# High scheduling priority for six DVE and ACT passes in a one-core, four-layer graph-network kernel

## The chip, the core and the metric

The kernel runs on one core of a Trainium2 chip. The metric is device time in microseconds (us) from launch to end; the median of three runs of the kernel before is 2236.18 us (2234.99 to 2238.05). The engines are TensorE (PE in the profile, with its weight loads shown as PEld), VectorE (DVE), ScalarE (ACT), GpSimd (POOL) and SyncE (SP). PE writes its products to PSUM, and DVE and ACT read them from there; POOL works in SBUF alone.

## The reference

128 graphs of 64 nodes with 256 features each go through four layers. Every layer ends in a residual and a LayerNorm.

```python
x = layernorm(x + L0(x, adj))   # five node groups (25, 9, 7, 6, 6 nodes): GCN 256->512->256, weighted sum
x = layernorm(x + L1(x, adj))   # D^-1/2 (adj + I) D^-1/2  x W + b
x = layernorm(x + L2(x, adj))   # sum_k conv_w[k] * An^k (x W^T) + conv_b, leaky ReLU; An = adj / row sum
x = layernorm(x + L3(x, adj))   # five rounds: m = h W_l; agg = A01^T m; h = GRU(agg, h)
```

Layer 2 is a polynomial in the normalised adjacency `An`. Layer 3 runs a gated recurrent cell five times: gates r and z are sigmoids, n is a tanh, and the new state is `(1 - z) n + z h`.

## The kernel before

**Tiling.** Layer 0 goes by 16 units of up to four tiles of graphs (`prep`, `aggregate`, `hidden`, `support`, `add`, `finish`). From layer 1 on the work goes by 16 chunks of eight graphs, held as four pairs of 128 nodes (`NP = 4`), so most tiles are 128 x 512 values of float32.

**Layers 1 and 2** of a chunk are the generator `mid(c)`. It builds `Ab` (two adjacencies as one block-diagonal 128 x 128), `An` and `dg` on DVE. Then it makes the layer-2 polynomial by Horner's rule: a transpose of `Ab` on PE (L255) and a DVE pass into `poly3` (L257); a product `An x poly` on PE into `pp` (L265) and a DVE pass that reads `pp` and writes `poly1` (L267); a second product on PE, with `poly1` as its operand (L272), and a DVE pass into `poly0` (L274). Between the two products stands `gather(xt, AT1)`: 16 matmuls into `pa` (L209) in two halves, each copied to SBUF by ACT (L212), and after it the DVE pass L269 on `xt`. A `yield` in `mid` marks where the caller may go on with something else.

**Layer 3** is the main loop over 80 steps (16 chunks of five rounds, two chunks in turn). A step `s` does the gates of one chunk (`x.rz`, `x.n`) while the other (`w`) finishes its round: `w.n(4)` and `w.n(3)` end in `update`, whose DVE passes L803 to L805 write the new state `hn`; `w.turn` transposes it on PE (L745) and `w.close` calls `messages`, which is `gather` into `agg` (L209, L212) and `sums` on POOL (`Ta`, L684 to L686; `Th` from `hn` in the same way). Each gate product is Strassen-like: seven products (numbers 1 to 7), whose partial sums in a PSUM bank are copied by ACT (L721) and added by DVE (L723, L727, L733). ACT then applies the sigmoids (L771, L773, L775) and the tanh (L802, in `update`). DVE's `reset` (L797, L798) stands in front of the tanh.

**What sets the order.** PE's order is written out by hand (`manual_schedule` for PE, L325): PE runs its instructions as the program text lists them. The order on DVE, ACT and POOL is chosen by a scheduler when the kernel is built: roughly, among the instructions that it takes as ready it issues the one that comes first in the program text, except that those traced under `tc.high_priority()` go first. Two passes have that priority already: the copies of partial sums (L721) and of the transposed state (L819). In layer 3 `next(filler)` runs one stage of `mid` of a later chunk in two places of each step, in PE's order after `x.rz(6)` and after `x.n(5)`. So the Horner stage (L265, gather, L272) falls between `x.rz(6)` and `x.rz(5)`, while DVE still works on `w.n(4)` and `w.n(3)`.

**PSUM.** Two pools: `pg` with five banks (gates) and `pt` with three (everything that `psum` allocates: `pT`, `pp`, `pa`, `pd`). The scheduler also decides which freed `pt` bank a new tile gets.

Of the kernel before, what the change touches and what calls it, by code (L numbers as in the profile page):

```python
# [11 lines left out]
ALU = mybir.AluOpType  # L12
# [55 lines left out]
def gnn_stack(  # L68
# [26 lines left out]
    nc = tc.nc  # L95
# [13 lines left out]
    def spread(src, n, name, pool=wp, eng=None):  # L109

        return const(bass.AP(tensor=src.tensor, offset=src.offset, ap=[[0, 128], [1, n]]), [128, n], name, eng, pool)

    powers, evictions = [], []

    def inv_sqrt(v, n, p, name):

        z = small.tile([p, n], F32, name=name + "z")
        nc.vector.tensor_scalar(z, v, 0.0, None, op0=ALU.is_equal)
        s = small.tile([p, n], F32, name=name + "s")
        nc.vector.tensor_add(s, v, z)  # L120
        r = small.tile([p, n], F32, name=name + "r")
        powers.append(nc.gpsimd.tensor_tensor(r, s, mhalf[:p, :n], ALU.pow))
        o = small.tile([p, n], F32, name=name + "o")
        nc.vector.scalar_tensor_tensor(o, v, 0.0, r, op0=ALU.not_equal, op1=ALU.mult)
        return o
# [51 lines left out]
    def psum(name):  # L177
        return pt.tile([128, 512], F32, tag="pt", name=name)

    def psum0(name):  # L180

        taken[0] += 1
        if taken[0] % 8 < 5:
            return pg.tile([128, 512], F32, tag="pg", name=name)
        return psum(name)
# [17 lines left out]
    def gather(src, m, name, pool=keep, tag="ag", bufs=1):  # L203

        a = pool.tile([128, 2, NP * 128], F32, tag=tag, name=name, bufs=bufs)
        for k in range(2):
            p = psum("pa")
            for q in range(NP):
                nc.tensor.matmul(  # L209
                    p[:, q * 128 : (q + 1) * 128], src[:, q, k * 128 : (k + 1) * 128], m[:, q, :], start=True, stop=True  # L210
                )
            nc.scalar.copy(a[:, k, :], p)  # L212
        return a

    adjs, xts = {}, {}
# [2 lines left out]
    def mid(c):  # L218
# [22 lines left out]
        dg = keep.tile([128, NP, 128], F32, name="dg", bufs=1)  # L241
# [3 lines left out]
        poly = keep.tile([128, NP, 128], F32, tag="poly", name="poly3", bufs=2)  # L245
# [7 lines left out]
        p = psum("pT1").rearrange("p (q n) -> p q n", q=NP)  # L253
        for q in range(NP):
            nc.tensor.transpose(p[:, q, :], Ab[:, q, :], ident)  # L255

        nc.vector.scalar_tensor_tensor(poly, p, cw[:, 3:4], poly, op0=ALU.mult, op1=ALU.add)  # L257

        nc.vector.tensor_add(AT1, p, ident[:, None, :].to_broadcast([128, NP, 128]))
        nc.vector.tensor_mul(AT1, AT1, dinv1[:, :, None].to_broadcast([128, NP, 128]))  # L260
# [2 lines left out]
        p = psum("pp").rearrange("p (q n) -> p q n", q=NP)  # L263
        for q in range(NP):
            nc.tensor.matmul(p[:, q, :], An[:, q, :], poly[:, q, :], start=True, stop=True)  # L265
        poly = keep.tile([128, NP, 128], F32, tag="poly", name="poly1", bufs=2)
        nc.vector.scalar_tensor_tensor(poly, dg, cw[:, 1:2], p, op0=ALU.mult, op1=ALU.add)  # L267
        ag = gather(xt, AT1, "ag1")
        nc.vector.tensor_add(xt, xt, l1bs[:, None, :].to_broadcast([128, NP, D]))  # L269
        p = psum("pp").rearrange("p (q n) -> p q n", q=NP)  # L270
        for q in range(NP):
            nc.tensor.matmul(p[:, q, :], An[:, q, :], poly[:, q, :], start=True, stop=True)  # L272
        poly = keep.tile([128, NP, 128], F32, tag="poly", name="poly0", bufs=2)
        nc.vector.scalar_tensor_tensor(poly, dg, cw[:, 0:1], p, op0=ALU.mult, op1=ALU.add)  # L274
        yield
        for u in range(NP // 2):
            p = psum("pd").rearrange("p (q d) -> p q d", q=2)
# [15 lines left out]


        ag = gather(xt, poly, "ag2")
        yield
        for u in range(NP // 2):
            p = psum("pd").rearrange("p (q d) -> p q d", q=2)
# [6 lines left out]
            v = keep.tile([128, 2, D], F32, name="v", bufs=1)  # L305
# [22 lines left out]
    with ExitStack() as c0:  # L328
# [29 lines left out]
        def prep(i):  # L358

            u = UNITS[i]  # L360
            a, xg = loads.pop(i)
            ae = work.tile([TR, 4, NJ], F32, name="ae", bufs=2)
            A0 = work.tile([TR, 4, TR], F32, name="A0", bufs=1)
            AT = work.tile([TR, 4, TR], F32, name="AT", bufs=4)
            p = psum0("pT").rearrange("p (t n) -> p t n", t=4)
            scale = []
            for ts, nb, r, k in u.same:
                w, c = ts.stop - ts.start, 0
                for f, m in [(0, u.n)] if u.g < 2 else RUNS[u.g]:
                    nc.vector.tensor_add(  # L370
                        ae[:r, ts, c : c + m], a[:r, ts, f : f + m], eye0[:r, k, None, c : c + m].to_broadcast([r, w, m])
                    )
                    c += m
                av = ae[:r, ts, : u.n]
                deg = small.tile([TR, w], F32, name="deg")
                nc.vector.tensor_reduce(deg[:r], av, AX.X, ALU.add)
                dinv = inv_sqrt(deg[:r], w, r, "d0")
                nc.vector.tensor_mul(av, av, dinv[:, :, None].to_broadcast([r, w, u.n]))
                o, c = 0, 0
                for _, m in RUNS[u.g]:  # L380
                    nc.vector.tensor_mul(
                        A0[:r, ts, o : o + nb * m].rearrange("p t (b n) -> p t b n", n=m),
                        ae[:r, ts, None, c : c + m].to_broadcast([r, w, nb, m]),
                        block0[:r, None, k, o : o + nb * m].rearrange("p t (b n) -> p t b n", n=m)
                        .to_broadcast([r, w, nb, m]),
                    )
                    o, c = o + nb * m, c + m
                for t in range(ts.start, ts.stop):
                    nc.tensor.transpose(p[:r, t, :r], A0[:r, t, :r], ident[:r, :r])
                scale.append((AT[:r, ts, :r], p[:r, ts, :r], dinv[:, :, None].to_broadcast([r, w, r])))  # L390
            for v in scale:
                evictions.append(nc.vector.tensor_mul(*v))
            A[i] = AT, xg

        def aggregate(i):
            u = UNITS[i]
            AT, xg = A[i]
            ag0 = work.tile([128, 2, 512], F32, name="ag0", bufs=2)
            for k in range(2):
                p = psum0("pa0")  # L400
                for t, r in enumerate(u.rows):
                    nc.tensor.matmul(  # L402
                        p[:, u.off[t] : u.off[t] + r], xg[:r, t, k * 128 : (k + 1) * 128], AT[:r, t, :r],
                        start=True, stop=True,
                    )
                nc.scalar.copy(ag0[:, k, : u.cols], p[:, : u.cols])
            AG[i] = ag0

        def hidden(i):
# [125 lines left out]
        def products(l, q):  # L535
# [7 lines left out]
            return p  # L543

        early = both(mid(0), mid(1))

        places = [(1, 1), (1, 2), (2, 1), (2, 2), (2, 2), (3, 1), (3, 2), (3, 2)]
# [11 lines left out]
        for i in range(-2, NU + 1):  # L559
# [3 lines left out]
            if i:  # L563
                stage(aggregate, i + 1)
            early_stage(i, 0)
            stage(support, i)
            if not i:
                aggregate(1)
# [4 lines left out]
            if i == -1:  # L573

                hidden(0)
                with tc.issue_after(evictions[0].ins):
                    prep(1)
            else:
                stage(prep, i + 2)
                stage(hidden, i + 1)  # L580
# [33 lines left out]
            elif i == 1:  # L614
                with tc.issue_after(powers[-1].ins):
                    pair = const_later(c_pair, [128, 2, N], "pair")
                    cw = spread(conv_w, 4, "cw", eng=nc.gpsimd)
# [117 lines left out]
    class Chunk:  # L735
# [20 lines left out]
        def messages(self, h=None):  # L756
            self.agg = gather(self.xt if h is None else h, self.A01, "agg", work, "agg", 2)
            self.ta = sums(self.agg, "a")
# [95 lines left out]
    for s in range(NCH * L):  # L854
        u, t = s // (2 * L) * 2, s % (2 * L)
        if t == 0:
            for _ in filler:
                pass
            if u + 2 < NCH:
                for c in (u + 2, u + 3):  # L860
                    load_adj(c)
                    load_x(c)
                filler = both(mid(u + 2), mid(u + 3))
# [104 lines left out]
```

## Time and profile before

| engine | busy us | share of the span |
|---|---|---|
| PE | 2184.9 | 98% |
| PEld | 1912.4 | 86% |
| DVE | 1402.4 | 63% |
| ACT | 1003.4 | 45% |
| POOL | 596.4 | 27% |

The profiled execution spans 2234.4 us and its mean granted PE clock is 0.995. PE is busy without a break over almost all of it, so the useful numbers are those of its idle time: 49.5 us in all (2234.4 less 2184.9). In time the kernel has a start-up of some 20 us, layer 0 until about 345 us, the main loop from there, in which `mid` runs beside layer 3 until about 1960 us, and a tail after PE's last long stretch at about 2200 us.

How to read the profile's lines. A row of the waits gives the engine and line that waited, whom it waited for, the total us, how many times, and the longest. A row of the timeline gives the start, the duration, the engine, the line of the kernel, the operation with output and inputs, how many instructions are merged, and in brackets how long the engine had been idle before it and what ended that. Instructions of DVE that follow each other overlap a little in such rows: one shown with 0.68 us is followed by the next 0.60 us after its start.

### The profile page before, as it was taken

The numbers are of one execution on the slowest core, as the hardware profiler recorded it, in microseconds if no ns is written. First come the engines' busy times: TensorE is split into PE (matmuls) and PEld (weight loads), VectorE is DVE, ScalarE is ACT, GpSimd is POOL, SyncE is SP. The second block draws the span as 40 slices with busy tenths as digits, with TensorE's granted clock in tenths as the row PEclk, the third lists the DMA queues.
The fourth block names the chain that finished last, engine by engine and source line by source line (L and its number), as shares of the span: only waits on it lengthen the run. The fifth ranks groups of instructions, "written<-read, shape, count | busy, mean of one in ns | idle before, by whom it ended". The sixth has DMA issues, their size and how long they took to land.

```text
span 2234.4 us, 30150 instructions
## 1 busy us (share of the span) xinstructions
PE 2184.9 (98%) x11526; PEld 1912.4 (86%) x11526; DVE 1402.4 (63%) x3068; ACT 1003.4 (45%) x1850; POOL 596.4 (27%) x639
## 2 busy tenths in 40 slices
PE   7999999999999999999999999999999999999997
PEld 5677788888888888888888888888888888888886
DVE  4443666675766666666756676757666666566546
ACT  2333334445545444445444454455454544455443
POOL 3210123222223223223222232222222232232222
PEclk9999999999999999999999999999999999999998
DMA  6531110000100000000100010001000000000000
GB/s 188 170 124 31 48 46 4 1 3 1 41 1 3 1 20 22 3 1 11 31 1 3 1 41 1 4 1 41 1 1 1 20 10 1 1 10 10 1 1 20
DMA packets 54172, 51.12 MB, mean 23 GB/s; under 512 B 20878, under 2 KB 49036, under 8 KB 54028
## 3 DMA queue, kind: packets, MB, share of 16 engines
q1 hardware_dynamic: 49524, 43.90, 6.4%
q0 software_dynamic: 1936, 4.83, 0.7%
q8 instruction: 91, 1.49, 0.3%
q10 hardware_dynamic: 2568, 0.47, 0.1%
q14 instruction: 53, 0.43, 0.1%
HBM read 32.40 MB, written 16.78 MB: 22 GB/s over the span
## 4 chain that ended last, share of the span: by engine, by line
PE 86%; DVE 7%; DMA 2%; issue 2%; POOL 1%; SPq 1%; ACT 0%; ACTq 0%; POOLq 0%; DVEq 0%
PE parz L704 23%; PE pdrz L704 12%; PE pan L704 12%; PE pa L209 8%; PE pdn L704 6%; PE pbrz L704 6%; PE pT L745 4%; PE pbn L704 3%; PE ph L416 3%; PE ps L430 3%; PE pd L281 2%; PE pd L302 2%; DMA xo<-in_x_dram 1%; PE pp L272 1%; PE pa L402 1%
## 5 line engine op out<-in xcount | busy, mean ns | idle before, releaser
L704 PE MATMUL parz<-Th,WHH 128*128 128x256 f32 x960 | 285.8, 379 | 0.0
L704 PE MATMUL parz<-Ta,V 128*128 128x256 f32 x960 | 285.5, 379 | 0.0
L684 POOL TENSOR_TENSOR Th<-hn 128x512 f32<-128x512 f32 x64 | 85.8, 1340 | 722.3 <-DVE hn L805 657.5
L721 ACT COPY c<-parz 128x512 f32<-128x512 f32 x240 | 140.8, 586 | 305.9 <-PE parz L704 305.1
L802 ACT ACTIVATE NI<-NI,bih 128x512 f32<-128x512 f32 x160 | 115.3, 721 | 224.3 <-DVE NI L798 224.3
L721 ACT COPY c<-pan 128x512 f32<-128x512 f32 x240 | 141.1, 588 | 150.7 <-PE pan L704 150.7
L704 PEld LDWEIGHTS parz<-Ta,V 128*128 128x128 f32 x960 | 182.4, 190 | 24.8
L684 POOL TENSOR_TENSOR Ta<-agg 128x512 f32<-128x512 f32 x80 | 104.6, 1307 | 345.4 <-ACT agg L212 345.4
L704 PEld LDWEIGHTS parz<-Th,WHH 128*128 128x128 f32 x960 | 176.2, 190 | 20.9 <-ACT c L721 0.2
L775 ACT ACTIVATE RZ<-RZ,brz 128x512 f32<-128x512 f32 x160 | 106.7, 714 | 138.3 <-DVE RZ L733 138.3
L733 DVE TENSOR_TENSOR RZ<-pdrz,c 128x512 f32<-128x512 f32 x80 | 55.0, 688 | 176.2 <-PE pdrz L704 176.2
L704 PE MATMUL pan<-Ta,V 128*128 128x256 f32 x480 | 143.1, 380 | 0.9 <-ACT c L721 0.9
L704 PE MATMUL pan<-Th,WHH 128*128 128x256 f32 x480 | 142.8, 379 | 0.0
L727 DVE TENSOR_TENSOR NI<-pbn,c 128x512 f32<-128x512 f32 x80 | 55.3, 692 | 127.7 <-PE pbn L704 125.3
L138 POOL TENSOR_TENSOR rs<-ve,mhalf 128x4 f32<-128x4 f32 (+2 forms) x66 | 68.1, 1032 | 242.9 <-DVE ve L136 235.6
L723 DVE TENSOR_TENSOR NI<-pdn,c 128x512 f32<-128x512 f32 x80 | 55.2, 689 | 115.3 <-ACT c L721 115.3
L209 PEld LDWEIGHTS pa<-A,h 128*128 128x128 f32 x1024 | 124.4, 192 | 3.3
L209 PE MATMUL pa<-A,h 128*128 128x128 f32 x1024 | 124.6, 275 | 0.0
L803 DVE TENSOR_TENSOR RZ<-hn,NI 128x512 f32<-128x512 f32 x128 | 87.9, 687 | 48.5 <-ACT NI L802 48.4
L805 DVE TENSOR_TENSOR hn<-RZ,NI 128x512 f32<-128x512 f32 x160 | 109.7, 686 | 1.8
L804 DVE TENSOR_TENSOR RZ<-RZ 128x512 f32<-128x512 f32 x160 | 109.5, 685 | 1.8
L797 DVE SCALAR_TENSOR_TENSOR NI<-NI,bhh,RZ 128x256 f32<-128x256 f32 (+1 forms) x160 | 105.1, 657 | 2.0
(199 smaller groups left out, 5107.6 us busy)
## 6 DMA issues: line engine op xcount, KB each, us to landing
out_dram<-xt SPq DMA_DIRECT2D x32, 256.0 KB
W<-in_w_dram SPq DMA_DIRECT2D x10, 512.0 KB
xt<-xb SPq DMA_DIRECT2D x32, 156.0 KB
xo<-in_x_dram SPq DMA_DIRECT2D x9, 512.0 KB
xb<-xo SPq DMA_DIRECT2D x9, 512.0 KB
xt<-xa SPq DMA_DIRECT2D x32, 100.0 KB
xg<-in_x_dram SPq DMA_DIRECT2D x25, 125.0 KB
xa<-xg SPq DMA_DIRECT2D x25, 125.0 KB
```

Source lines behind the costliest of these rows:

```text
L138: nc.gpsimd.tensor_tensor(rs[:r, :n], ve[:r, :n], mhalf[:r, :n], ALU.pow)
L209: nc.tensor.matmul(p[:, q * 128 : (q + 1) * 128], src[:, q, k * 128 : (k + 1) * 128], m[:, q, :], start=True, stop=True)
L684: nc.gpsimd.tensor_sub(t[:, 0:2, :], a[:, :, H:], a[:, 0, :].rearrange("p (s n) -> p s n", s=2))
L704: nc.tensor.matmul(bank[:, g, :], w[:, q, i - 1, :], rhs, start=i in (1, 2, 5) and g == 0 and m == 0, stop=m == len(side) - 1, skip_group_ ...
L721: nc.scalar.copy(c, self.a)
L745: nc.tensor.transpose(p[:, q * 128 : (q + 1) * 128], src(q, k), ident)
L775: nc.scalar.activation(RZ[:, q, 0, :], RZ[:, q, 0, :], AF.Sigmoid, bias=b[0])
L797: nc.vector.scalar_tensor_tensor(n[:, j, f], h, bhh[:, 4 + j : 5 + j], r[:, j, f], op0=ALU.add, op1=ALU.mult)
L802: nc.scalar.activation(n, n, AF.Tanh, bias=bih[:, 4 + j : 5 + j])
L803: nc.vector.tensor_sub(d, self.hT[:, j, :], n)
L804: nc.vector.tensor_mul(d, d, z)
L805: nc.vector.tensor_add(self.hn[:, j, :], d, n)
```

## The change

Six passes are put under `tc.high_priority()`: the ACT copies of `gather` (L212) and layer 0's `aggregate` (L406), the three polynomial passes on DVE that read PSUM (L257, L267, L274), and the scaled transposes of layer 0 (L392). The result of each is an operand of a later PE instruction. Nothing is computed differently, no instruction is added or removed, and no buffer is resized. PE's order is the same in both kernels; only the places of instructions on DVE, ACT and POOL, and with them which of the three `pt` banks a tile gets, can differ.

```diff
@@ gather
-            nc.scalar.copy(a[:, k, :], p)
+            with tc.high_priority():
+                nc.scalar.copy(a[:, k, :], p)
@@ mid
-        nc.vector.scalar_tensor_tensor(poly, p, cw[:, 3:4], poly, op0=ALU.mult, op1=ALU.add)
+        with tc.high_priority():
+            nc.vector.scalar_tensor_tensor(poly, p, cw[:, 3:4], poly, op0=ALU.mult, op1=ALU.add)
...
-        nc.vector.scalar_tensor_tensor(poly, dg, cw[:, 1:2], p, op0=ALU.mult, op1=ALU.add)
+        with tc.high_priority():
+            nc.vector.scalar_tensor_tensor(poly, dg, cw[:, 1:2], p, op0=ALU.mult, op1=ALU.add)
...
-        nc.vector.scalar_tensor_tensor(poly, dg, cw[:, 0:1], p, op0=ALU.mult, op1=ALU.add)
+        with tc.high_priority():
+            nc.vector.scalar_tensor_tensor(poly, dg, cw[:, 0:1], p, op0=ALU.mult, op1=ALU.add)
@@ prep
             for v in scale:
-                evictions.append(nc.vector.tensor_mul(*v))
+                with tc.high_priority():
+                    evictions.append(nc.vector.tensor_mul(*v))
@@ aggregate
-                nc.scalar.copy(ag0[:, k, : u.cols], p[:, : u.cols])
+                with tc.high_priority():
+                    nc.scalar.copy(ag0[:, k, : u.cols], p[:, : u.cols])
```

## The prediction

> **What bounds the kernel now.** I read the busy table first: PE 98%, everything else at 63% or less. So the end is set by PE's work plus PE's idle time, and a change of order can only act on the idle time. The second view is the busy time by stage, in whose rows the columns are the stretch, its length, and then PE, PEld, DVE, ACT and POOL.
>
> ```profile
> 0.00:20.00 20.00, 8.45 (x25) 5.81 (x26) 8.32 (x30) 2.53 (x4) 9.60 (x18) 1.00 0.83 225
> 20.00:200.00 180.00, 171.71 (x818) 127.43 (x817) 76.30 (x326) 62.78 (x107) 38.00 (x44) 0.98 0.40 125
> 200.00:360.00 160.00, 155.75 (x830) 129.22 (x829) 98.95 (x286) 57.34 (x125) 37.44 (x50) 0.99 0.15 44
> 360.00:1921.00 1561.00, 1550.84 (x8314) 1385.94 (x8313) 1033.63 (x2071) 735.16 (x1349) 428.50 (x440) 1.00 0.03 10
> 1921.00:2180.00 259.00, 259.00 (x1355) 230.51 (x1354) 149.42 (x276) 126.50 (x231) 69.80 (x76) 1.00 0.02 5
> 2180.00:2234.40 54.40, 39.14 (x194) 33.49 (x192) 35.79 (x82) 19.06 (x34) 13.05 (x12) 0.88 0.06 20
> ```
>
> Length less PE gives PE's idle time: 11.6 at the start, 8.3 and 4.2 in layer 0 and the passage to layer 3, 10.2 in the main loop while `mid` runs, 0.0 in the loop without it, 15.3 in the tail: 49.5 us. The third view says whom PE waits for.
>
> ```profile
> PE pp L272 <- DVE rinv L236: 8.5, 10, 1.5
> PE pa L402 <- DVE AT L392: 7.4, 4, 2.9
> PE pp L272 <- DVE mv L134: 1.7, 2, 1.2
> PE pp L272 <- ACT NI L802: 1.4, 1, 1.4
> PE ph L416 <- ACT ag L406: 1.3, 1, 1.3
> PE pp L272 <- DVE poly L267: 0.2, 1, 0.2
> ```
>
> The second Horner product (L272) has 8.5 + 1.4 + 0.2 = 10.1 us of it, which is all of the main loop's 10.2, and 1.7 in layer 0. The releaser named, `rinv` or `NI`, is not its input: L272 needs `poly1` of L267, and the instruction named merely ended last. The timeline of one such place shows it.
>
> ```profile
> 612.55 1.95 PE L209 MATMUL pa<-AT,xt 128*128 128x128 f32 x16
> 613.88 0.67 DVE L805 TENSOR_TENSOR hn<-RZ,NI 128x512 f32<-128x512 f32 x1
> 614.48 0.68 DVE L798 TENSOR_TENSOR NI<-NI 128x512 f32<-128x512 f32 x1
> 615.09 0.73 DVE L267 SCALAR_TENSOR_TENSOR poly<-dg,cw,pp 128x512 f32<-128x512 f32 x1
> 615.19 0.72 ACT L802 ACTIVATE NI<-NI,bih 128x512 f32<-128x512 f32 x1 [0.97 <-DVE NI L798]
> 615.96 1.13 PE L272 MATMUL pp<-poly,An 128*128 128x128 f32 x8 [1.47 <-DVE rinv L236]
> ```
>
> L267 ends at 615.82 and PE starts 0.14 later. Its input `pp` was complete by 612.7 (L265 starts at 611.65 and takes 1.05). So it stood more than 2 us behind DVE passes of the gates.
>
> **What the skill says.** The Trainium skill, "Perfetto Trace Analysis", section "Tensor Engine Instruction (MATMUL, LD_WEIGHTS)", has ACT, DVE and GPSIMD as strict FIFOs: a ready pass waits for whatever stands ahead. The stretch above agrees: DVE is busy without a gap and L267 starts 2.4 us after its input was there. "SBUF — State Buffer", section "SBUF: two separate sides", says that DVE and GpSimd share a pair of ports under an exclusive lock, so that one blocks the other for a whole instruction. The trace agrees: L118, a pass over 128x4 that takes 0.17 us elsewhere, took 1.14 at 620.78, while POOL's `Th` (L684, 1.59 us from 620.31) ran. I use this below for what the later `hn` does to POOL.
>
> **The change part by part.** I compared the built order of both kernels. PE's and SP's are identical.
>
> *L267 in the main loop (14 chunks).* It moves ahead of one pass, L798, and so starts 0.60 us earlier (614.48 in place of 615.09). The waits at L272 alternate in the two chunks of a pair: 1.47 (at 616) and 0.24 (at 712). Over seven pairs they are none and 0.24, five times 1.47 and 0.24, then 1.42 and none: 10.2 us. A wait of 0.24 goes entirely, one of 1.47 becomes 0.87, since L797 and L805 still stand ahead. Gain: 6 x 0.60 + 6 x 0.24 = 5.0 us.
>
> *L267 in layer 0 (two chunks).* It moves from behind four and three LayerNorm statistics to behind the first; at 278 that is from 277.76 to about 276.6, so it ends about 277.3, when PE is through with `pa` (278.62 less the 1.23 of its wait). Both waits, 0.51 and 1.23, go: 1.7 us. Its neighbours L153 and the stores of `xg` come about 1.5 us later there. DVE then waits 4.6 us for PE before L286 at 288.44, which hides this.
>
> *L274* moves ahead of L803 and L804. `poly0` is read by `gather` more than 20 us later: nothing gained. What is queued behind both passes: L798, and with it the tanh L802 and the second ACT copy of `pa`, 0.6 us later, and L805 for `hn`, which also falls behind L248, 0.6 us later. Readers: PE's transpose L745 of that half at 623.41, when `hn` was written by 620.2; 3.2 us of slack shrink to about 2. `pa`'s second half is read by L281 at 629.96. POOL's `Th` starts 0.6 later and in five chunks has a 1.0 us `d1r` put in between; it is needed together with `Ta`, which POOL starts only at 629.74. L723 at 621.91 can lose about 0.4 us to the port lock; its bank is written again at 624.72. Cost on PE: zero, 1 us at most per pair.
>
> *L212 for `agg` (78 moves of L775).* The order r, z, copy, copy becomes r, copy, copy, z. The copies end about 0.5 us earlier, but PE has no wait on `Ta` or `agg` in the loop, so nothing is gained. The sigmoid z (L775) is later by some 1.1 us; it is read by L804 in the next step, some 10 us on. The ACT copy behind it waits for PE anyway: 1.42 us at 2196.00 in a step without `mid`, 1.39 us at 655.29 in one with it, which is more than z's delay. In the 14 closing rounds L150 also moves behind the copies; the sum ahead of the `pan` copy stays. Cost: zero.
>
> *L406* does not move at all: the 1.3 us stay. *L392* moves in four units, all after 205 us, where PE does not wait for it; the waits of 7.4 us lie before 130 us and those passes keep their places. *L257* moves by one 0.08 us pass once. Zero each.
>
> *Banks.* L272's bank is now the one that L267 frees, where before it was one freed by an ACT copy; that copy had ended by 614.23 and did not bind. The transposes take the ACT-freed bank, 5 us later. Zero.
>
> Sum: 5.0 + 1.7 = 6.8 us; 2236.2 - 6.8 = **2229.4**.
>
> **The rivals.** (1) *Given back*: PE comes to each later place up to 0.6 us earlier while DVE, ACT and POOL have the same backlog; a wait on `hn`, on the copy of `h` (ready 1.5 us ahead of L209 at 626.44) or on a reused bank takes over. For it: DVE is gapless from 607 to 622 there. Against it: no such wait is among PE's rows, and the slacks are 1.5 us or more. If two thirds of the loop's 5.0 go, the gain is 1.7 + 1.7 = 3.4: 2232.8. (2) *All bubbles go*, because the port lock and ACT's queue resolve better as well: 10.2 + 1.7 = 11.9, so 2224.3. Against it: two long passes stay ahead of L267. (3) *Slower*: the later z or tanh makes each of the 78 reordered steps wait 0.15 us in ACT's queue at a `pan` copy, +11.7 - 6.8 = +4.9: 2241.1. For it: it would happen in every step. Against it: the 1.4 us that ACT waits for PE there, and PE's 0.0 us of idle in 259 us of loop without `mid`.
>
> **How the numbers follow.** Forecast 0.66 (2228 to 2231, with the 0.1% that the runs of before differ), rival 1 0.20, rival 2 0.06, rival 3 0.08. The range 2226 to 2235.5 takes in the forecast and rival 1 and leaves out most of the others. Over 0.2% is 4.5 us: the forecast clears it by 2.3 us, a run's spread, so I give it 0.62 of its 0.66 and some of rival 1; faster 0.73. Within 0.2%: 0.19. Slower: 0.08.
>
> **What would show it.** In the changed profile the rows of PE's waits for L272 should sum to about 5.2 us (six of 0.87) in place of 11.9, the main loop's PE idle to 5, and layer 0's two to nothing; the waits of L402 on AT stay at 7.4. L775 z stands behind the copies. A new PE row with L745, L209 or L704 waiting for DVE or ACT in the loop, in tens of times, would show rival 1 or 3.

## The result, and the profile after

The changed kernel takes 2219.03 us (median of six runs, 2217.32 to 2220.84); before, measured with it, takes 2238.31 (2234.99 to 2242.37). The ratio is 0.9914, with an interval of 0.9902 to 0.9927; a second measurement gave 2222.08 us and 0.9924 (0.9912 to 0.9937). The forecast was 2229.4 and its range ended at 2226.0: the direction was right, but the gain is 16 to 19 us where 6.8 were forecast.

**Line numbers after.** The added `with` lines shift the numbers in the profile of after. Those used below, before and after: L212 is L213, L224 is L225, L257 is L259, L260 is L262, L267 is L270, L272 is L275, L381 is L385, L389 is L393, L392 is L397, L402 is L407, L406 is L412, L416 is L422, L684 to L686 are L690 to L692, L704 is L710, L745 is L751, L775 is L781, L797 and L798 are L803 and L804, L805 is L811. L150 keeps its number. The views below show chosen rows; those between them are left out.

Busy time by stage of after (stretch, length, PE, PEld, DVE, ACT, POOL), against the rows of before with the same stretches:

```profile
200.00:360.00 160.00, 157.18 (x837) 130.62 (x836) 98.81 (x286) 57.33 (x125) 38.14 (x50) 0.99 0.15 44
360.00:1921.00 1561.00, 1561.00 (x8395) 1398.77 (x8394) 1018.58 (x2089) 743.24 (x1363) 417.81 (x443) 1.00 0.03 10
1921.00:2180.00 259.00, 259.00 (x1358) 231.09 (x1357) 146.62 (x270) 127.52 (x233) 70.64 (x77) 1.00 0.02 5
```

PE's idle time in the main loop went from 10.2 us to nothing. Look at the other columns of that row as well: DVE's busy time fell by 15 us (1033.63 to 1018.58) and POOL's by 10.7 (428.50 to 417.81), although in after slightly more of their instructions fall into this stretch (2089 for 2071, and 443 for 440). A mere change of order doesn't shorten passes; this is the first sign of what the prediction missed. PE's four largest waits of after:

```profile
PE pT L393 <- DVE A L385: 10.0, 1, 10.0
PE pa L407 <- DVE AT L397: 6.4, 4, 2.6
PE pT L751 <- DVE hn L811: 5.4, 2, 4.1
PE ph L422 <- ACT ag L412: 4.1, 1, 4.1
```

No row for the second Horner product (L275) is left, and none of the loop's gates has come in. The place that the prediction showed, in the timeline of after:

```profile
610.43 1.05 PE L267 MATMUL pp<-poly,An 128*128 128x128 f32 x8
611.22 0.68 DVE L811 TENSOR_TENSOR hn<-RZ,NI 128x512 f32<-128x512 f32 x1
611.82 0.73 DVE L270 SCALAR_TENSOR_TENSOR poly<-dg,cw,pp 128x512 f32<-128x512 f32 x1
612.48 0.68 DVE L804 TENSOR_TENSOR NI<-NI 128x512 f32<-128x512 f32 x1
613.11 0.61 PE L275 MATMUL pp<-poly,An 128*128 128x128 f32 x4
```

The order is the predicted one: `hn`, the polynomial pass, then L804. But the pass starts 1.39 us after the first product (611.82 less 610.43) where before it was 3.44 (615.09 less 611.65). One place in the order is worth 0.60 of these 2.05 us. DVE's whole backlog is shorter by about 1.4 us.

**Where the time came from.** PE runs the same 11526 matmuls in the same order in both kernels, so the distances from each matmul's start to the next can be compared one by one. In the loop (by before's times, from 345 to 2180 us) they add up to 15.4 us less:

| place in the loop | us | occurrences |
|---|---|---|
| last L209 to first L272 | 12.43 | 14 |
| first to second matmul of L272 (184 ns to 112 ns) | 1.01 | 14 |
| `parz` products on `agg` in closing rounds | 1.92 | 8, two steps each |

Layer 0's two waits at L272 add 2.0 us (1.94 to the first matmul, 0.04 inside). Other differences in layer 0 come and go between runs of the same kernel, by 2 to 3 us. The second measurement of the changed kernel has 12.43, 1.02 and 1.92 in the loop, so these terms can be relied on.

**What the prediction didn't see.** A closing round is one in which a finished chunk leaves layer 3 and a new one enters. The one ahead of the place above, first before (DVE, ACT and POOL rows of the timeline):

```profile
602.29 2.07 ACT L150 ACTIVATE xt<-xt,nb,rs 128x256 f32<-128x256 f32 x4
604.27 1.04 ACT L212 COPY agg<-pa 128x512 f32<-128x512 f32 x2
605.35 0.68 DVE L224 TENSOR_TENSOR Ab<-a,pair 128x512 f32<-128x512 f32 x1
605.39 1.77 POOL L684 TENSOR_TENSOR Ta<-agg 128x512 f32<-128x512 f32 x1 [3.33 <-ACT agg L212]
605.95 1.76 DVE L260 TENSOR_TENSOR AT<-AT,d1o 128x512 f32<-128x512 f32 x1
607.24 1.05 POOL L685 TENSOR_TENSOR Ta<-agg,Ta 128x256 f32<-128x256 f32 x1
608.37 0.86 POOL L686 TENSOR_TENSOR Ta<-agg,Ta 128x256 f32<-128x256 f32 x1
608.56 0.94 DVE L797 SCALAR_TENSOR_TENSOR NI<-NI,bhh,RZ 128x256 f32<-128x256 f32 x1
```

and then after:

```profile
600.33 1.05 ACT L213 COPY agg<-pa 128x512 f32<-128x512 f32 x2
601.46 1.29 POOL L690 TENSOR_TENSOR Ta<-agg 128x512 f32<-128x512 f32 x1 [0.64 <-ACT agg L213]
601.90 2.07 ACT L150 ACTIVATE xt<-xt,nb,rs 128x256 f32<-128x256 f32 x4
604.12 0.80 DVE L225 TENSOR_TENSOR Ab<-a,pair 128x512 f32<-128x512 f32 x1
604.84 0.68 DVE L262 TENSOR_TENSOR AT<-AT,d1o 128x512 f32<-128x512 f32 x1
606.38 0.47 DVE L803 SCALAR_TENSOR_TENSOR NI<-NI,bhh,RZ 128x256 f32<-128x256 f32 x1
```

Before, the copies of `agg` stand behind four LayerNorm passes of the finished chunk, so POOL's `Ta` begins only at 605.39, while DVE is at L224 and has L260, the second pass on `AT1`, next. `Ta`'s three passes take 1.77, 1.05 and 0.86 us in place of 1.29, 0.73 and 0.73; L260 takes 1.76 in place of 0.68, and L797, beside `Ta`'s last pass, 0.94 in place of 0.47. The ends fit a lock held for whole instructions: POOL's first pass, stretched beside L224, ends at 607.16, and DVE's 0.68 us pass, issued at 605.95, ends 0.55 later at 607.71. This is the rule of the Trainium skill ("SBUF — State Buffer", "SBUF: two separate sides") that the prediction used only for `Th`. After, the copies go first, `Ta` is through at 604.37, before L262 comes, and that pass takes 0.68 us in all 16 chunks. Before, it took 1.76 in six, 1.21 in six others, and 0.68 in the first three and the last.

In each of the six worst chunks the step from one DVE pass to the next shrinks by 1.08 us at L260 and by 0.47 at L797, and grows by 0.11 at L224, which now meets the end of `Ta`: 1.44 us together, the shorter backlog found above.

The third term was visible as well, in a view that the prediction left out. Waits of the weight-load queue (PEld) before, and one of the eight places in the timeline of before:

```profile
PEld parz L704 <- ACT agg L212: 3.0, 8, 0.4
```

```profile
582.35 1.04 ACT L212 COPY agg<-pa 128x512 f32<-128x512 f32 x2
582.40 0.59 PE L704 MATMUL parz<-hT,WHH 128*128 128x256 f32 x2
582.97 0.70 PE L704 MATMUL parz<-agg,V 128*128 128x256 f32 x2
```

The matmuls that read `agg` wait for the copy of 582.35. PE's own rows show no idle time there, because the modelled end of the product in front (582.99) lies past the start of the next.

### The profile page after: what moved, and what is told of

Read it like the earlier page. It is cut to its first block, busy times and chain, and to the rows that moved or that the text cites. A ratio compares the mean times of both kernels' runs of the same rounds, so it can differ in the third digit from the quotient of the medians.

```text
span 2218.8 us, 30141 instructions
## 1 busy us (share of the span) xinstructions
PE 2180.1 (98%) x11526; PEld 1912.2 (86%) x11526; DVE 1376.3 (62%) x3068; ACT 1004.5 (45%) x1850; POOL 582.5 (26%) x639
## 4 chain that ended last, share of the span: by engine, by line
PE 91%; DMA 3%; DVE 2%; issue 1%; SPq 1%; POOL 1%; ACT 0%; POOLq 0%; ACTq 0%; DVEq 0%
PE parz L710 25%; PE pdrz L710 12%; PE pan L710 12%; PE pa L209 9%; PE pbrz L710 6%; PE pdn L710 6%; PE pT L751 4%; PE pbn L710 3%; PE ph L422 3%; PE ps L436 3%; PE pd L285 2%; PE pd L306 2%; DMA xo<-in_x_dram 1%; PE pa L407 1%; PE po L458 1%
## 5 line engine op out<-in xcount | busy, mean ns | idle before, releaser
L710 PE MATMUL parz<-Th,WHH 128*128 128x256 f32 x960 | 285.8, 379 | 0.0
L710 PE MATMUL parz<-Ta,V 128*128 128x256 f32 x960 | 285.5, 379 | 0.0
L690 POOL TENSOR_TENSOR Th<-hn 128x512 f32<-128x512 f32 x64 | 81.6, 1274 | 774.0 <-DVE hn L811 588.5
L710 PEld LDWEIGHTS parz<-Ta,V 128*128 128x128 f32 x960 | 182.4, 190 | 24.7
L710 PEld LDWEIGHTS parz<-Th,WHH 128*128 128x128 f32 x960 | 176.2, 190 | 20.9 <-ACT c L727 0.2
L781 ACT ACTIVATE RZ<-RZ,brz 128x512 f32<-128x512 f32 x160 | 116.1, 727 | 138.6 <-DVE RZ L739 138.6
L690 POOL TENSOR_TENSOR Ta<-agg 128x512 f32<-128x512 f32 x80 | 102.2, 1277 | 260.6 <-ACT agg L213 260.6
L710 PE MATMUL pan<-Ta,V 128*128 128x256 f32 x480 | 143.2, 380 | 0.9 <-ACT c L727 0.9
L710 PE MATMUL pan<-Th,WHH 128*128 128x256 f32 x480 | 142.7, 379 | 0.0
L209 PEld LDWEIGHTS pa<-A,h 128*128 128x128 f32 x1024 | 124.4, 192 | 3.3
L209 PE MATMUL pa<-A,h 128*128 128x128 f32 x1024 | 124.6, 275 | 0.0
L811 DVE TENSOR_TENSOR hn<-RZ,NI 128x512 f32<-128x512 f32 x160 | 109.9, 687 | 1.8
L436 PE MATMUL ps<-W,hg 128*125 128x256 f32 (+5 forms) x464 | 104.2, 382 | 0.0
```

The source lines that it names most:

```text
L209: nc.tensor.matmul(p[:, q * 128 : (q + 1) * 128], src[:, q, k * 128 : (k + 1) * 128], m[:, q, :], start=True, stop=True)
L436: nc.tensor.matmul(p[: u.rows[t], t - v, :], hg[:, e, u.off[t] : u.off[t] + u.rows[t]], W2[:, u.g, e, :], start=e == 0, stop=e == 3,)
L690: nc.gpsimd.tensor_sub(t[:, 0:2, :], a[:, :, H:], a[:, 0, :].rearrange("p (s n) -> p s n", s=2))
L710: nc.tensor.matmul(bank[:, g, :], w[:, q, i - 1, :], rhs, start=i in (1, 2, 5) and g == 0 and m == 0, stop=m == len(side) - 1, skip_group_ ...
L781: nc.scalar.activation(RZ[:, q, 0, :], RZ[:, q, 0, :], AF.Sigmoid, bias=b[0])
L811: nc.vector.tensor_add(self.hn[:, j, :], d, n)
```

## The experiments

Two theories at first. A: the polynomial passes carry the whole gain, and the copies nothing, as the prediction has it. B: the copies' order sets when `Ta` runs, `Ta` slows DVE's `AT1` pass, and this delay is what keeps L267 late. Losses at L272 are from start to start, against the 0.11 us that the step takes in after.

**The polynomial passes alone** (`e1_poly`; L257, L267, L274). The edit against the whole change:

```diff
-            with tc.high_priority():
-                nc.scalar.copy(a[:, k, :], p)
+            nc.scalar.copy(a[:, k, :], p)
...
-                with tc.high_priority():
-                    evictions.append(nc.vector.tensor_mul(*v))
+                evictions.append(nc.vector.tensor_mul(*v))
...
-                with tc.high_priority():
-                    nc.scalar.copy(ag0[:, k, : u.cols], p[:, : u.cols])
+                nc.scalar.copy(ag0[:, k, : u.cols], p[:, : u.cols])
```

> Before, with the priority on the three polynomial passes alone (L257, L267, L274); ACT's order stays that of before. Theory A (the gain of the whole change comes from the place of the polynomial passes): nearly all of the 19 us, about 2220; L272 no longer waits. Theory B (half of it comes from the copies of agg, which let POOL make Ta before DVE's pass on AT1, so that the two do not block each other): AT1's pass keeps its 1.76 and 1.21 us, the long stalls at L272 shrink by 0.60 each to about 1.0 and the short ones go; 6 x 0.60 + 6 x 0.40 + some 0.9 of restarts = 6.9 us in the loop and about 1.9 in layer 0, so 8.8 less than before.

Measured: 2229.2 us (2225.57 to 2230.72), ratio 0.9955 (0.9942 to 0.9967). The row of PE's waits for the second product (L274 in this kernel):

```profile
PE pp L274 <- DVE poly L269: 4.6, 6, 0.8
```

Six waits of 0.77 stay, close to the six of 0.87 that the prediction left; the other places' small ones are gone. The `AT1` pass still takes 1.76 and 1.21. From start to start the loop gains 7.3 us, all at L272, and layer 0's two places there 1.9. Theory A falls. That the time is the one predicted for the *whole* change, 2229.4, is partly luck: the gain is 9.0 us in place of 6.8, from a before that was 2.0 us slower beside these runs than the 2236.2 of the forecast. The three passes weren't tried one by one.

**The copies of `gather` alone** (`e2_gather`; L212 with priority, the other five passes as before). The edit against before:

```diff
-            nc.scalar.copy(a[:, k, :], p)
+            with tc.high_priority():
+                nc.scalar.copy(a[:, k, :], p)
```

> Before, with the priority on the ACT copies of gather (L212) alone; DVE's order stays that of before, and L267 stays behind L798. Theory A: no gain, since PE has no visible wait on agg or Ta. Theory B: every pass on AT1 takes 0.68 us in place of 1.76 and 1.21; L267 comes 1.45 us earlier in six chunks and 0.53 in six others; 6 x 1.45 + 6 x 0.40 + 1.9 (the products on agg that follow a closing round) = 13.0 us in the loop, nothing in layer 0.

Measured: 2226.72 us (2224.87 to 2227.88), ratio 0.9946 (0.9933 to 0.9958). In the loop the part that the prediction costed at zero is worth more than the part that it costed, 11.9 us (10.0 at L272, 1.9 at `parz`) against 7.3. The `AT1` pass takes 0.68 us in every chunk, and layer 0's two waits stay at 1.7.

**Layer 0's passes alone** (`e3_layer0`; L392 and L406), against before:

```diff
             for v in scale:
-                evictions.append(nc.vector.tensor_mul(*v))
+                with tc.high_priority():
+                    evictions.append(nc.vector.tensor_mul(*v))
...
-                nc.scalar.copy(ag0[:, k, : u.cols], p[:, : u.cols])
+                with tc.high_priority():
+                    nc.scalar.copy(ag0[:, k, : u.cols], p[:, : u.cols])
```

> Before, with the priority on the two passes of layer 0 alone (L392, L406). Both theories: nothing beyond the spread of runs; the four waits of L402 on AT keep their 7 us, since the passes that move stand after 205 us. A third theory, that these passes bring the part of the gain that the main loop does not show, expects 3 to 4 us less than before.

Measured: 2238.02 us (2235.85 to 2241.33), ratio 1.0001 (0.9993 to 1.0009): nothing, as predicted. The third theory falls.

**`Ta` made late again** (`e4_late_ta`): the whole change, and at the first messages of a chunk two small POOL passes (1.99 us together) that read `agg` and stand ahead of `Ta`:

```diff
             self.agg = gather(self.xt if h is None else h, self.A01, "agg", work, "agg", 2)
+            if h is None:
+                for i in range(2):
+                    d = small.tile([128, NP], F32, name="dly")
+                    nc.gpsimd.tensor_tensor(d, self.agg[:, 1, :NP], mhalf[:, :NP], ALU.pow)
             self.ta = sums(self.agg, "a")
```

> The whole change, with two small POOL passes (128x4, about 1.0 us each, result unused) put ahead of Ta in the 16 places where a chunk enters layer 3; all other orders are those of the change. Ta is then made some 2 us later in these places, as before the change. Theory A: no difference from the whole change, since Ta has slack. Theory B: POOL and DVE block each other again at AT1's pass (over 1.2 us in six chunks), L267 comes later by 1 to 1.5 us there, and L272 waits again in these six by up to about 1.0 us: up to 6 us more than the whole change.

Measured: 2225.34 us (2223.89 to 2226.59), ratio 0.9939 (0.9926 to 0.9953), against 0.9914 and 0.9924 of the whole change. The timeline of this kernel shows the collision again, with `Ta`'s second pass now, and its waits show the product waiting again:

```profile
606.57 1.05 POOL L691 TENSOR_TENSOR Ta<-agg,Ta 128x256 f32<-128x256 f32 x1
606.96 1.21 DVE L262 TENSOR_TENSOR AT<-AT,d1o 128x512 f32<-128x512 f32 x1
```

```profile
PE pp L275 <- DVE poly L270: 1.1, 6, 0.2
```

ACT's copies were as early as in the whole change; only POOL's time moved. So it is `Ta`, not ACT's order as such, that holds the chain at L272. The collision is milder (1.21 in place of 1.76), and so is the loss: 2.7 us in the loop, all at L272, with the 1.9 at `parz` kept.

**Only the 14 closing rounds** (`e5_closing`): before, with priority for the `agg` copies of a new chunk alone. DVE's, POOL's and PE's orders are those of before; on ACT 28 copies pass one z and four L150 passes.

```diff
-    def gather(src, m, name, pool=keep, tag="ag", bufs=1):
+    def gather(src, m, name, pool=keep, tag="ag", bufs=1, first=False):
...
-            nc.scalar.copy(a[:, k, :], p)
+            with tc.high_priority() if first else nullcontext(): nc.scalar.copy(a[:, k, :], p)
...
-            self.agg = gather(self.xt if h is None else h, self.A01, "agg", work, "agg", 2)
+            self.agg = gather(self.xt if h is None else h, self.A01, "agg", work, "agg", 2, h is None)
```

> Priority for the copies of `agg` (L212) in the 14 closing rounds that hand a new chunk over to layer 3, and for nothing else: in the built order 28 copies on ACT pass one sigmoid z and the four L150 passes, and every other instruction of every engine keeps its place, DVE's all included. Theory B (POOL's `Ta` of these 14 rounds runs into DVE's `AT1` pass, because its input is copied late): the same gain as with all of L212's copies, some 12 us in the loop, so about 2226 us, with the `AT1` pass L260 at 0.68 us everywhere and no wait of 1 us or more left at L272. Theory A (the order of the copies is worth nothing, as the prediction has it): 2238. Theory D (each of the 78 displaced sigmoids and the copies of `mid` is worth a share): 14 of 78, some 2 us: 2236.

Measured: 2227.24 us (2223.64 to 2229.35), ratio 0.9948 (0.9935 to 0.996). The loop gains 10.6 us (8.63 at L272, all in the six chunks that lost 1.6 each, and 1.92 at `parz`). Theory B holds for these, and D's share of 2 us falls, but B's text was too strong in one point: the `AT1` pass stays at 1.21 in the other six chunks. The round that these six meet lies inside the other chunk, so its copies have no priority in this kernel and stay behind r and z (the two L775 passes from 694.48). That one z ahead of the copies is enough:

```profile
694.48 1.33 ACT L775 ACTIVATE RZ<-RZ,brz 128x512 f32<-128x512 f32 x2 [1.87 <-DVE RZ L733]
695.72 1.05 ACT L212 COPY agg<-pa 128x512 f32<-128x512 f32 x2
698.97 0.68 DVE L224 TENSOR_TENSOR Ab<-a,pair 128x512 f32<-128x512 f32 x1
699.01 1.23 POOL L686 TENSOR_TENSOR Ta<-agg,Ta 128x256 f32<-128x256 f32 x1
699.57 1.21 DVE L260 TENSOR_TENSOR AT<-AT,d1o 128x512 f32<-128x512 f32 x1
```

`Ta`'s last pass meets L224, waits for it, and makes L260 wait in turn. With all copies ahead of z (`e2_gather`) the same three `Ta` passes begin 0.6 us sooner after r, and L260 takes 0.68. That is the 1.4 us by which `e2_gather`'s loop beats this one's: 6 x 0.24, again from copies costed at zero.

**The polynomial passes and the closing rounds** (`e6_poly_closing`; the two edits above together, here two of the added lines):

```diff
+        with tc.high_priority(): nc.vector.scalar_tensor_tensor(poly, p, cw[:, 3:4], poly, op0=ALU.mult, op1=ALU.add)
...
+            with tc.high_priority() if first else nullcontext(): nc.scalar.copy(a[:, k, :], p)
```

> Priority for the three polynomial passes (L257, L267, L274) and for the `agg` copies of the 14 closing rounds; the other 64 places of the `agg` copies, `mid`'s gathers, L392 and L406 stay as before. Theory B: that is the whole change, 2217 to 2221 us, with PE never waiting in the loop while `mid` runs. Theory D: the 64 other places are worth something too, so this is slower than the whole change by 5 us or more, about 2225.

Measured: 2222.16 us (2219.94 to 2224.33), ratio 0.9927 (0.9915 to 0.994). The whole change beside it on the same chip (`e5_whole`) gave 2222.08 (2219.19 to 2222.62).

> The whole change once more, to be compared on one chip with the three kernels beside it. Every theory expects what it gave before, 2217 to 2221 us.

Both are 1 us above the expected 2217 to 2221. The two are equal, and term by term in the trace as well: 12.43, 1.01 and 1.92 in the loop. The `AT1` pass still takes 1.21 in the other six chunks, but there L267 ends 0.34 us or more before L272 starts, which doesn't wait. Once L267 has its priority, the 64 other places of the `agg` copies and `mid`'s copies are worth nothing, and layer 0's passes nothing either.

**Two misses on the waits that are left.** Layer 0's AT passes (L397) wait on DVE behind LayerNorms of `others`. `e7_others_later` issues these after the AT pass:

```diff
-                        f(o)
+                        with tc.issue_after(evictions[-1].ins) if f is others and i >= 0 else nullcontext(): f(o)
```

> The whole change, and from layer 0's third round on the LayerNorm of the nodes outside the five groups (`others`) is issued on DVE only after the scaled transposes (`AT`) of the same round. In before and after alike those transposes stand behind DVE LayerNorm passes that wait for a load, and PE waits 6.4 us for them in four places. If these waits are worth their length, 6 us less than the whole change: about 2213 us. If layer 0 is held by its loads, another wait takes their place: 2217 to 2221 as the whole change.

Measured: 2231.0 us (2229.57 to 2234.54), ratio 0.997 (0.9957 to 0.9982), 9 slower than the whole change beside it. PE waits 14.2 us for AT and 5.8 for `s` (L442). A row of SyncE's waits suggested a reason: a store stands first in the queue until the late LayerNorm is through.

```profile
SPq L520 <- DVE mv L134: 17.3, 1, 17.3
```

But this wait ends at 208.21, and PE's large waits for AT end earlier, 8.5 us at 96.72 and 4.5 at 143.26. The row can't be their cause. No store waits more than 0.3 us in the queue before 133 us.

`e8_store_later` also moves the first seven of the ten stores back by a round:

```diff
-                    if min(o + 1, 9) == j:
+                    if min(o + 1, 9) + (f is store_others and o < 7) == j:
```

> As the run before this one (the whole change, `others` issued on DVE after the scaled transposes of the round), and the store of each normalised `xo` moved one round later in SyncE's queue. There the stores had waited 17 us for the later LayerNorms, with the loads of the next unit queued behind them. If that queue was what cost 9 us against the whole change, the loss goes and PE's waits for AT (L397) shrink below the 6.4 to 9.0 us of the whole change: 2213 to 2219 us. If the loads are late for another reason, it stays near 2231.

Measured: 2230.24 us (2226.55 to 2231.3), ratio 0.9966 (0.9952 to 0.9979). PE still waits 10.9 us for AT and 5.6 for `s`. The row above stands in this trace too, with its 17.3 us, since its store is not among the seven; so the run says nothing about that store. What does hold layer 0 here wasn't settled. Neither kernel beats the whole change, and `e6_poly_closing` only equals it.

## Why the prediction was wrong, step by step

*L267's own term* was right in mechanism and about right in size. It moved one place, 0.60 us, and with the copies left alone six waits stayed. The 7.3 us of `e1_poly` against 5.0 has two causes. The rows of waits list 10.1 us at L272 in the loop, but the starts show 12.4, and a product that had to wait takes 0.07 more for its second matmul: each of the 14 places costs some 0.2 us more than its listed wait, and in `e1_poly` eight of them stop waiting. The six that go on waiting start 0.69 us earlier in place of 0.60, since PE starts 0.09 us sooner after L267's end (last section).

*The step that failed* is the one on L212: "PE has no wait on `Ta` or `agg` in the loop, so nothing is gained". It is wrong twice. First, PE's weight loads did wait for `agg`, 3.0 us in eight places by their own row, 1.92 from start to start; the prediction's "everything else at 63% or less" passed over their 86%. Second and larger, it gave the copies 0.5 us, though in the closing rounds, with four L150 passes moved behind them, they come 2.7 us earlier, and the reasoning stopped at the direct readers of `Ta`. POOL's time for `Ta` also decides how long a DVE pass takes, and that pass stands ahead of L267. The prediction had the lock in hand, applied it to the later `hn` and `Th`, and did not ask which DVE passes `Ta` ran into *before*; the 1.76 of L260 beside its 0.68 elsewhere would have told.

*How the two parts add up.* By the trace, in one of the six worst chunks L267 ended 1.48 us after PE was ready for L272. Its place in DVE's order gives 0.60, the lock 1.44; together 2.04, so 0.56 is left over as slack (measured in after, in these six: 0.55 to 0.58). The place alone leaves 0.88 (measured in `e1_poly`: 0.87 to 0.88 in five, 0.84 in the last), the copies alone 0.04 (measured in `e2_gather`: 0.02 to 0.05). The parts overlap: 7.3 and 11.9 us alone, 15.4 together.

*Layer 0's L267*: 1.7 predicted, 2.0 measured. *L274, L392, L406 and the later z* at zero: right; no new row of waits came in. The wait behind L406, which was to stay at 1.3 us, is 4.1 and 3.5 in the two runs of the whole change. ACT's order in `e3_layer0` is that of before, so the priority of L406 moves nothing; in the other kernels, with it or without, the wait is 0.4 to 2.9. *Banks* at zero: right for the whole change, where no product of L272 waits in the loop; the 0.09 us of `e1_poly` come with the other bank. *L402's waits* stay, 6.4 to 9.0 in two runs of the same kernel.

*The rivals.* Giving back and z's delay didn't happen. The second rival named the real cause ("the port lock and ACT's queue resolve better as well") but was given 6 in 100 because "two long passes stay ahead of L267": they do, and they come 1.4 us earlier. Even it was short, 11.9 us for 17.4, by what the rows of waits do not list.

## What to carry to other kernels

When a pass moves on one engine, follow it through every engine that its result starts, and ask what *runs beside* that work before and after, not only who reads it: a producer that starts 2.7 us earlier, seen from PE's work (605.39 to 611.65 against 601.46 to 610.43), can shorten another engine's pass. Passes of one shape with two or three durations in the trace are the place to look; here 0.68, 1.21 and 1.76 us. And read the waits of PE's weight loads as well as PE's, and distances from start to start where the stalls are short.

## What was not expected of the hardware

A DVE pass of 0.68 us between two POOL passes took 1.21 or 1.76, and the POOL passes stretched too (0.73 to 1.05 or 1.23, 1.29 to 1.77): each waited for the other's instruction to end. After L267's end, PE started L272 146 ns later where L272's bank had been freed by ACT (before, `e2_gather`) and 55 ns later where L267 itself had freed it (the whole change's banks, read in `e1_poly` and `e4_late_ta`), although ACT had been done before. In the first case the weight load waits for a semaphore of ACT as well as one of DVE, in the second for DVE's alone; whether that is the cause wasn't tested by itself. A PE product restarted after a stall took 184 to 213 ns to its second matmul in place of 112.
